# A graph kernel with attention: four attention tiles in one span of 68 nodes, softmax masks computed once

## The chip, the cores and the metric

The kernel runs on one core of a Trainium2 chip. The metric is the device time of one launch in microseconds (us), the median of several runs. The core has a matrix engine (PE; its weight loads are listed as PEld), VectorE (DVE), ScalarE (ACT), GpSimd (POOL) and SyncE (SP), each with its own instruction stream. SBUF is the working memory of 128 partitions, PSUM the memory that PE writes to.

## What is computed

A graph of 6250 nodes with 128 features and 100,000 edges, sorted by target, passes through a layer norm and two relational layers (RGCN), is added to the input, passes through a second layer norm and two attention layers (GAT) with batch norm and ELU, and is added again. The change concerns the attention layers:

```python
def _gat(x, src, dst, W, a_src, a_dst, b):        # H = 4 heads of FH = 32
    n = x.shape[0]
    xw = (x @ W).reshape(n, H, FH)
    al_s = jnp.einsum('nhf,hf->nh', xw, a_src)
    al_d = jnp.einsum('nhf,hf->nh', xw, a_dst)
    e = jax.nn.leaky_relu(al_s[src] + al_d[dst], NEG_SLOPE)
    m = jax.ops.segment_max(e, dst, num_segments=n)
    ee = jnp.exp(e - m[dst])
    den = jax.ops.segment_sum(ee, dst, num_segments=n)
    alpha = ee / den[dst]
    out = jax.ops.segment_sum(alpha[:, :, None] * xw[src], dst, num_segments=n)
    return out.reshape(n, H * FH) + b
...
loops = jnp.arange(n, dtype=edge_index.dtype)     # every node also has an edge to itself
src = jnp.concatenate([edge_index[0], loops])
dst = jnp.concatenate([edge_index[1], loops])
```

## The kernel before

**Tiles and chunks.** The 106,250 edges with self-loops, sorted by target, are cut into 832 tiles of 128 edges (`NT`), one edge a partition, and into 26 chunks of 32 tiles (`NCH`, `TC`). A table in device memory has a row for each node: 128 projected features and 2 x 4 attention terms (`DG` = 136 numbers). In `gat`, `gathers(k)` fetches the rows of a chunk's sources, one indirect DMA on POOL for each tile (L584), into two buffers of 16 tiles from the pool `grp` of seven.

**Sums.** `sums(k)` works through a chunk two tiles at a time, in 16 steps. `weight` (L917) multiplies the gathered rows of four tiles by their softmax weights `w`. `selections` (L601) makes for eight tiles a matrix of zeros and ones, 128 edges by a window of `W` = 24 nodes: `window == offset`, where `offset` is an edge's target less the first target of its tile. The matmul of rows and selection (L937) gives 128 features x 24 nodes in PSUM; `add` (L921) adds this to the running sum `self.sum` at a column that is known only at run time, so the first targets of the tiles (`base`, `start`) are read into VectorE's registers by `bases` (L589), 16 at a time. Before the first tile of a chunk the column of the node that is shared with the chunk before is corrected by the factor `shrink` (L930, L931). A tile that spans more than 24 nodes would need more passes of the loop in `layer`; their number (`passes_g`) is computed from the data.

**Softmax.** `softmax(k)` has a chunk as 128 partitions (4 heads x 32 tiles) by 128 edges. It copies the attention terms out of the gathered rows (ACT, L797), transposes them (L799), and finds each target's maximum and sum along the edges by scans in both directions. The masks for this are made anew in each chunk from `rows`, the targets as numbers: `cut` is 0 where neighbouring edges share the target and very negative else (L787 to L789), `same` is cut == 0 (L791), and `dr == dr[:, c]` finds the edges that share the target of the first or last edge of a tile (L823, L900). Targets that run over tile borders are joined by short scans over the 32 tiles on 4 partitions (L811 to L890), whose carries from chunk to chunk are copied into fresh tiles (`dl`, `ml`, `sc`). `own_tile` (L436, L437) picks for each partition the value of its own tile, by a product and a reduction.

**Order.** `in_order` fixes the traced order within DVE, ACT, PE and POOL. In the loop of `gat`, the gathers of chunk k+1 are issued ahead of the sums of chunk k, and the softmax of chunk k+1 is a generator whose steps are interleaved with the second half of the sums of chunk k: one step at step 3 (the masks) and one at each of the steps 7 to 15. So VectorE's queue has, behind the early half of the sums, the softmax of the next chunk, which waits for the last gather of that chunk.

**Lists.** `windows` and `chains` compute the graph's lists (`base`, `ahead`, the link masks) once. They run as steps between the halves of the first RGCN layer, as `early` in `run`. The RGCN layers have their own gathers (`htable`, 782 a layer, also L584), selections (L698, L703) and additions (L749).

Of the kernel before, what the change touches and what calls it, by code (L numbers as in the profile page):

```python
# [8 lines left out]
F32 = mybir.dt.float32  # L9
I32 = mybir.dt.int32  # L10
BF16 = mybir.dt.bfloat16
AF = mybir.ActivationFunctionType
# [32 lines left out]
NZ = -(-(N + 1) // W)  # L45
WG = 288
# [5 lines left out]
BIG = 1e30  # L52

# [14 lines left out]
class Gnn:  # L68
# [251 lines left out]
    order = staticmethod(lambda v: v.rearrange("o (c p) -> o p c", p=NP))  # L320
    by_tile = staticmethod(lambda v: v.rearrange("o (p c) -> o p c", c=SC))

    def windows(self, scratch):

        nc, const, dst = self.nc, self.const, self.dst
        order, by_tile = self.order, self.by_tile
        self.base = const.tile([1, NT], I32, name="base")
        nc.vector.tensor_copy(by_tile(self.base), order(dst[0:1, :]))  # L330
        self.ahead = const.tile([P, NT], F32, name="ahead")
        last, firsts, lasts = scratch[:, :NT], scratch[:, NT:2 * NT], scratch[:, 2 * NT:3 * NT + 1]
        flags = scratch[:, 4 * NT:6 * NT].rearrange("o (i t) -> o i t", i=2)
        for c in range(0, NT, NT // 2):
            w = slice(c, c + NT // 2)
            ps = self.ps()[:, :NT // 2]
            nc.tensor.matmul(ps, self.ones, dst[0:1, w], start=True, stop=True)
            nc.vector.scalar_tensor_tensor(self.ahead[:, w], ps, -1.0, dst[:, w], op0=ALU.mult, op1=ALU.add)
            ps = self.ps()[:, :NT // 2]
            nc.tensor.matmul(ps[:1, :], self.ident[:, P - 1:P], dst[:, w], start=True, stop=True)  # L340
            nc.vector.tensor_copy(last[:, w], ps[:1, :])
        yield
        nc.vector.tensor_copy(by_tile(firsts), order(dst[0:1, :]))
        nc.vector.memset(lasts[:, 0:1], -1.0)
        nc.vector.tensor_copy(by_tile(lasts[:, 1:]), order(last))
        nc.vector.tensor_tensor(flags[:, 0, :], firsts, lasts[:, :NT], ALU.is_equal)
        nc.vector.tensor_tensor(flags[:, 1, :], firsts, lasts[:, 1:], ALU.is_equal)

        nc.vector.tensor_sub(lasts[:, 1:], lasts[:, 1:], firsts)
        widest = scratch[:, 0:1]  # L350
        nc.vector.tensor_reduce(widest, lasts[:, 1:], AX.X, ALU.max)
        steps = self.small.tile([1, NZ], F32, name="steps", bufs=1)
        nc.vector.tensor_scalar(steps, self.steps, widest, None, op0=ALU.is_le)
        count = self.small.tile([1, 1], F32, name="count", bufs=1)
        nc.vector.tensor_reduce(count, steps, AX.X, ALU.add)
        passes = const.tile([1, 1], I32, name="passes")
        nc.vector.tensor_copy(passes, count)
        self.passes_g = passes
        yield

        self.both = const.tile([H, 2, NT], BF16, name="both")
        for i in range(2):
            for c in range(0, NT, NT // 2):
                w = slice(c, c + NT // 2)
                ps = self.ps()[:, :NT // 2]
                nc.tensor.matmul(ps[:H, :], self.ones[:, :H], flags[:, i, w], start=True, stop=True)
                nc.vector.tensor_copy(self.both[:, i, w], ps[:H, :])
        yield

    def chains(self, scratch):  # L370
# [3 lines left out]
        link, one = chunked(self.both[:, 0, :]), chunked(self.both[:, 1, :])  # L374
        self.link = link
        wide = [H, NCH, TC + 1]

        self.linkpen = const.tile(wide, BF16, name="linkpen")
        nc.vector.memset(self.linkpen, -BIG)
        lk = chunked(scratch[:H, NCH * P:NCH * P + NT])  # L380
        nc.vector.tensor_scalar(lk, link, 1.0, BIG, op0=ALU.subtract, op1=ALU.mult)
        nc.vector.tensor_copy(self.linkpen[:, :, :TC], lk)
# [3 lines left out]
        self.through = const.tile(wide, BF16, name="through")  # L386
        nc.vector.memset(self.through, 0.0)
        nc.vector.tensor_mul(self.through[:, :, 1:], link, one)
        self.throughpen = const.tile(wide, BF16, name="throughpen")
        nc.vector.tensor_scalar(self.throughpen, self.through, 1.0, BIG, op0=ALU.subtract, op1=ALU.mult)  # L390
        yield

        self.back = const.tile(wide, BF16, name="back")
        nc.vector.memset(self.back, 0.0)
        nc.vector.tensor_mul(self.back[:, :, :TC - 1], one[:, :, :TC - 1], link[:, :, 1:])
        self.apart = const.tile([H, NCH, TC], BF16, name="apart")
        nc.vector.tensor_scalar(self.apart, one, -1.0, 1.0, op0=ALU.mult, op1=ALU.add)
        self.backpen = const.tile(wide, BF16, name="backpen")
        nc.vector.memset(self.backpen, -BIG)
        nc.vector.tensor_scalar(self.backpen[:, :, :TC], one, 1.0, BIG, op0=ALU.subtract, op1=ALU.mult)  # L400
        nc.vector.tensor_add(self.backpen[:, :, :TC - 1], self.backpen[:, :, :TC - 1], self.linkpen[:, :, 1:TC])
        yield


        self.rows = const.tile([P, NCH, P], F32, name="rows")
        ri = scratch[:, :NCH * P].bitcast(I32).rearrange("p (k e) -> p k e", e=P)
        kv = self.keys[:NT * P].rearrange("(k t e) -> t k e", t=TC, e=P)
        for h in range(H):
            nc.sync.dma_start(ri[h * TC:(h + 1) * TC], kv)
        for k in range(0, NCH, 2):  # L410
            yield
            nc.vector.tensor_scalar(ri[:, k:k + 2], ri[:, k:k + 2], KDST, None, op0=ALU.logical_shift_right)
            nc.vector.tensor_scalar_mul(self.rows[:, k:k + 2], ri[:, k:k + 2], BIG)

# [805 lines left out]
```

## Time and profile before

| what | us |
|---|---|
| median of 3 runs (lowest, highest) | 4509.92 (4507.43, 4512.96) |
| the profiled execution: its time, its span | 4509.92, 4502.3 |
| gathers of RGCN layer one and two, first to last | 62.2 to 1050.0, 1086.4 to 2066.1 |
| gathers of attention layer one and two, first to last | 2165.5 to 3245.8, 3333.9 to 4415.5 |
| ACT, busy in all | 475.6 (11% of the span) |
| RECIPROCAL L895, one of 52 | 0.944 |
| DMA, mean share of 16 engines in 3334 to 3900 us | 0.23 |

The span is the time from the first to the last instruction of one profiled execution; the rest of its time lies around it. "Busy" adds up the time in which an engine executes. In the groups, a line of the program, an engine and an operation stand with their count, busy time and the mean of one, and behind the bar the engine's idle time just before them with what ended it. The granted clock of PE is 0.75 to 0.78 of full speed in the RGCN stretches and 0.50 in the attention.

### The profile page before, as it was taken

The numbers are of one execution on the slowest core, as the hardware profiler recorded it, in microseconds if no ns is written. First come the engines' busy times: TensorE is split into PE (matmuls) and PEld (weight loads), VectorE is DVE, ScalarE is ACT, GpSimd is POOL, SyncE is SP. The second block draws the span as 40 slices with busy tenths as digits, with TensorE's granted clock in tenths as the row PEclk, the third lists the DMA queues.
The fourth block names the chain that finished last, engine by engine and source line by source line (L and its number), as shares of the span: only waits on it lengthen the run. The fifth ranks groups of instructions, "written<-read, shape, count | busy, mean of one in ns | idle before, by whom it ended". The sixth has DMA issues, their size and how long they took to land. (4 is left out here: it accounts for less than half of the span.)

```text
span 4502.3 us, 41706 instructions
## 1 busy us (share of the span) xinstructions
PE 2645.9 (59%) x10042; PEld 2039.6 (45%) x10042; DVE 2567.8 (57%) x8572; ACT 475.6 (11%) x683; POOL 3153.1 (70%) x3242
## 2 busy tenths in 40 slices
PE   4888788887886888886244444444334344444434
PEld 3655555555555555554243333334323333333433
DVE  6556665554555555554365566556546556655656
ACT  3111110112110101102100000000030000000002
POOL 3777777775777777772577777777627777777771
PEclk8777787776777777777555555555555555555555
DMA  4221222222222222221222222222212222222221
GB/s 117 65 61 52 57 67 54 53 54 73 68 60 81 53 54 54 54 53 33 59 55 54 54 54 54 54 54 54 46 52 55 54 54 54 54 54 54 55 54 42
DMA packets 135172, 256.85 MB, mean 57 GB/s; under 512 B 56018, under 2 KB 76486, under 8 KB 134917
## 3 DMA queue, kind: packets, MB, share of 16 engines
q0 software_dynamic: 103296, 218.57, 19.9%
q1 hardware_dynamic: 31388, 34.67, 2.4%
q8 instruction: 88, 1.44, 0.1%
q14 instruction: 168, 1.37, 0.1%
q10 hardware_dynamic: 232, 0.80, 0.1%
HBM read 236.45 MB, written 17.37 MB: 56 GB/s over the span
## 5 line engine op out<-in xcount | busy, mean ns | idle before, releaser
L584 POOL DMA_INDIRECT v<-gtable,src_i x1664 | 1655.4, 995 | 694.0 <-issue 476.0
L584 POOL DMA_INDIRECT v<-htable,src_e x1564 | 1489.1, 952 | 567.7 <-issue 445.7
L740 PE MATMUL ps<-sw,v 128*128 128x192 f32 x3128 | 925.9, 423 | 293.2 <-DMA v<-htable,src_e 258.9
L740 PEld LDWEIGHTS ps<-sw,v 128*128 128x128 f32 x3128 | 587.6, 227 | 583.3 <-DMA v<-htable,src_e 303.8
L937 PE MATMUL ps<-sel,v 128*128 128x24 f32 x3328 | 772.1, 385 | 91.7 <-DVE v L917 65.4
L937 PEld LDWEIGHTS ps<-sel,v 128*128 128x128 f32 x3328 | 747.4, 330 | 139.5 <-DVE v L917 71.1
L749 DVE TENSOR_TENSOR part<-part,ps 128x192 f32 x1564 | 552.2, 353 | 272.2 <-PE ps L740 197.7
L711 PE MATMUL ps<-part,basis 128*128 128x288 f32 x1568 | 538.7, 511 | 2.3 <-DVE part L749 2.3
L799 PE MATMUL ps<-ident,sd 128*128 128x128 f32 x104 | 46.1, 475 | 768.4 <-ACT sd L797 768.4
L711 PEld LDWEIGHTS ps<-part,basis 128*128 128x128 f32 x1568 | 383.9, 252 | 122.8 <-issue 2.8
L804 DVE SCALAR_TENSOR_TENSOR own<-cut,ps 128x128 f32<-128x128 f32 x52 | 14.9, 287 | 657.5 <-PE ps L799 657.5
L706 ACT COPY part<-zero 128x2304 f32<-128x2304 f32 x100 | 210.9, 2111 | 1597.8 <-PE ps L711 1578.2
L799 PEld LDWEIGHTS ps<-ident,sd 128*128 128x128 f32 x104 | 19.0, 182 | 786.7 <-ACT sd L797 786.7
L921 DVE TENSOR_TENSOR acc<-acc,ps 128x24 f32 x1664 | 295.1, 177 | 101.4 <-PE ps L937 48.9
L703 DVE TENSOR_TENSOR sw<-sel,ps 128x1536 f32<-128x1536 f32 x196 | 343.7, 1754 | 13.0 <-DVE sel L698 0.2
L716 DVE TENSOR_TENSOR acc<-acc,ps 128x288 f32 x98 | 44.5, 454 | 458.3 <-PE ps L711 458.3
L917 DVE TENSOR_TENSOR v<-v,w 128x512 f32<-128x512 f32 x416 | 286.0, 687 | 5.0 <-ACT w L908 1.7
L797 ACT COPY sd<-v 128x64 f32<-128x64 f32 x208 | 53.0, 301 | 1162.6 <-DMA v<-gtable,src_i 1162.6
L430 PE MATMUL ps<-sel,head_of 128*4 128x32 f32 x208 | 44.6, 313 | 178.1 <-DVE sel L428 178.1
L892 PE MATMUL ps<-part,of_head 4*128 4x65 f32 x104 | 35.6, 443 | 171.1 <-DVE part L890 171.1
L691 PE MATMUL ps<-relT,of_tile 8*128 8x128 f32 x392 | 98.0, 331 | 51.7 <-DMA relT<-rels 51.7
L695 PEld LDWEIGHTS ps<-wc,hot 128*128 128x128 f32 x392 | 94.8, 260 | 40.0 <-DVE hot L692 39.7
(293 smaller groups left out, 2050.3 us busy)
## 6 DMA issues: line engine op xcount, KB each, us to landing
v<-gtable,src_i POOLq DMA_INDIRECT x1664, 2.6
v<-htable,src_e POOLq DMA_INDIRECT x1564, 2.5
gtable<-gtb SPq DMA_DIRECT2D x14, 476.0 KB
acc<-htable SPq DMA_DIRECT2D x24, 256.0 KB
htable<-x SPq DMA_DIRECT2D x7, 448.0 KB
relT<-rels SPq DMA_DIRECT2D x196, 4.0 KB
htable<-y SPq DMA_DIRECT2D x7, 448.0 KB
x<-in_x_dram SPq DMA_DIRECT2D x7, 441.0 KB
```

The source lines that it names most:

```text
L584: self.nc.gpsimd.indirect_dma_start(out=out, out_offset=None, in_=table, in_offset=bass.IndirectOffsetOnAxis(ap=idx, axis=0))
L691: nc.tensor.matmul(ps[:, :P], self.of_tile, rel.pop(h), start=True, stop=True)
L695: nc.tensor.matmul(coef[h][:, P:P + SC * NBASE], t, wc.rearrange("p g b -> p (g b)"), start=True, stop=True)
L703: nc.vector.tensor_tensor(x, s[:, :, None, :].to_broadcast(shape), c[:, :, :, None].to_broadcast(shape), ALU.mult)
L706: nc.scalar.copy(x, self.zero[:, :, None].to_broadcast([P, NBASE, WG]))
L711: nc.tensor.matmul(ps[:, :WG], bs[:, b, :], x[:, b, :], start=b == 0, stop=b == NBASE - 1)
L740: nc.tensor.matmul(ps[:, (j - i) * NBASE * W:(j - i + 1) * NBASE * W], v[:, i0 + j, :], sw[h][:, j].rearrange("p b w -> p (b w)"), start=T ...
L749: nc.vector.tensor_add(o, o, x.rearrange("p (b w) -> p b w", b=NBASE))
L799: nc.tensor.transpose(ps[:, i * P:(i + 1) * P], st.rearrange("p h t -> p (h t)"), self.ident)
L917: nc.vector.tensor_mul(x, x, wz[:, :, :, None].to_broadcast([P, Q, H, FH]))
L921: nc.vector.tensor_add(o, o, ps[:, j * W:(j + 1) * W])
L937: nc.tensor.matmul(ps[:, j * W:(j + 1) * W], v[i // G][:, i % G, :D], s[:, i % GD, :], start=True, stop=True)
```

## The change

1. A span of `WA` = 68 nodes takes the place of the 24-node window in the attention. Four tiles (`GQ`) share it: their offsets are counted from the first target of the four, their matmuls add up in one PSUM bank, and one addition of 128 x 68 follows them in place of four of 128 x 24. `weight` takes eight tiles at once instead of four; a selection is 8 x 68 wide. The registers are read once for a chunk, nine of them.
2. `cut`, `same`, `head` and `tail` are computed once for all chunks, in `chains`, as 16-bit floats and bytes, and kept; `softmax` reads them. `rows` and `rowlink` are no longer kept.
3. The chains over the tiles run on in one array (`ends`, 2 x 833 on 4 partitions): a chunk's scan starts from the element before it, with no copies of carries. The backward scans have two arrays in turn (`backs`). The two corrections at a tile's ends become one product.
4. `shrink` is copied by ACT. The softmax has nine steps instead of ten. The pool `grp` has six buffers instead of seven.

The diff, cut to its core:

```diff
+GQ = 4
+WA = 68
+NZA = -(-(N + 1) // WA)
...
     def windows(self, scratch):
...
+        for q in range(NQ):
+            first = dst[0:1, q * GQ * NP:(q * GQ + 1) * NP]
+            nc.vector.tensor_copy(self.base[:, :, q], first)
+            ps = self.ps()[:, :NP]
+            nc.tensor.matmul(ps, self.ones, first, start=True, stop=True)
...
+            nc.vector.tensor_sub(of_group(self.ahead[:, w]), of_group(dst[:, w]), ps[:, None, :].to_broadcast([P, GQ, NP]))
...
     def chains(self, scratch):
...
+        self.cut = tile("cut", P, P + 1)
+        self.same, self.head, self.tail = (tile(name, P, P, dtype=U8) for name in ("same", "head", "tail"))
...
         for k in range(0, NCH, 2):
+            z = slice(k, k + 2)
             yield
...
+            nc.vector.tensor_sub(self.cut[:, z, 1:P], rows[:, z, :P - 1], rows[:, z, 1:])
+            for mask, e in ((self.head, 0), (self.tail, P - 1)):
+                nc.vector.tensor_tensor(mask[:, z], rows[:, z], rows[:, z, e:e + 1].to_broadcast([P, 2, P]), ALU.is_equal)
...
+            nc.vector.tensor_scalar(self.same[:, z], self.cut[:, z, :P], 0.0, None, op0=ALU.is_equal)
...
+    def selections(self, g):
+
+        s = self.wide.tile([P, GD, WA], F32, name="selg")
         self.nc.vector.tensor_tensor(
-            s, self.window[:, None, :].to_broadcast([P, GD, W]),
-            self.offset[:, c:c + (GD - 1) * NP + 1:NP, None].to_broadcast([P, GD, W]), ALU.is_equal)
+            s, self.window[:, None, :].to_broadcast([P, GD, WA]),
+            self.offset[:, g:g + (GD - 1) * NP + 1:NP, None].to_broadcast([P, GD, WA]), ALU.is_equal)
...
     def softmax(self, k):
...
-        cut = self.soft.tile([P, P + 1], F32, name="cut")
-        nc.vector.tensor_copy(cut[:, 0:1], self.rowlink[:, k:k + 1])
-        nc.vector.memset(cut[:, P:], 0.0)
-        nc.vector.tensor_sub(cut[:, 1:P], dr[:, :P - 1], dr[:, 1:])
-        same = t("same")
-        nc.vector.tensor_scalar(same, cut[:, :P], 0.0, None, op0=ALU.is_equal)
-        yield
+        cut, same = self.cut[:, k, :], self.same[:, k, :]
...
-        nc.vector.tensor_copy(dl[:, 1:], cps[:H, :TC])
-        nc.vector.tensor_copy(dl[:, 0:1], carry[0])
...
+        nc.vector.tensor_tensor_scan(dc[:, past], ahead, cps[:H, :TC], dc[:, k * TC:k * TC + 1], op0=ALU.mult, op1=ALU.add)
...
-        nc.vector.tensor_scalar(e, dr, dr[:, 0:1], dcol, op0=ALU.is_equal, op1=ALU.mult)
-        nc.vector.tensor_add(e, e, d)
+        nc.vector.scalar_tensor_tensor(e, self.head[:, k, :], dcol, d, op0=ALU.mult, op1=ALU.add)
...
-        for i, c in enumerate((0, P - 1)):
-            self.own_tile(cols[:, i:i + 1], ps[:, i * TC:(i + 1) * TC])
-            nc.vector.tensor_scalar(inv, dr, dr[:, c:c + 1], cols[:, i:i + 1], op0=ALU.is_equal, op1=ALU.mult)
-            nc.vector.scalar_tensor_tensor(e, inv, 1.0, e, op0=ALU.add, op1=ALU.mult)
-        self.shrink = self.chain.tile([P, 1], F32, name="shrink")
-        nc.vector.tensor_copy(self.shrink, ps[:, 2 * TC:2 * TC + 1])
+        nc.scalar.copy(self.shrink, ps[:, 2 * TC:2 * TC + 1])
+        self.own_tile(cols, ps[:, :2 * TC].rearrange("p (i t) -> p i t", i=2))
+        nc.vector.tensor_scalar(inv, self.head[:, k, :], cols[:, 0:1], 1.0, op0=ALU.mult, op1=ALU.add)
+        nc.vector.scalar_tensor_tensor(inv, self.tail[:, k, :], cols[:, 1:2], inv, op0=ALU.mult, op1=ALU.add)
+        nc.vector.tensor_mul(e, e, inv)
...
     def sums(self, k, w, shrink):
...
+            x = v[t // G][:, t % G:t % G + GD, :D].rearrange("p t (h f) -> p t h f", h=H)
+            wz = w[:, :, t:t + GD].rearrange("p h t -> p t h")
+            nc.vector.tensor_mul(x, x, wz[:, :, :, None].to_broadcast([P, GD, H, FH]))
+        def add(i, ps):
+            o = self.sum[:, bass.ds(at[i], WA)]
+            nc.vector.tensor_add(o, o, ps[:, :WA])
         weight(0)
+        at = self.registers(self.start[0:1, k, :])
...
+            if t % GQ == 0:
+                ps = self.ps()
+            for i in range(t, t + 2):
+                nc.tensor.matmul(ps[:, :WA], v[i // G][:, i % G, :D], s[:, i % GD, :],
+                                 start=i % GQ == 0, stop=i % GQ == GQ - 1)
+            if t % GD == 0:
+                g = (k * TC + t) // GD + 1
+                if g < NT // GD:
+                    self.s = self.selections(g)
+                if t + GD < TC:
+                    weight(t + GD)
             if late:
                 add(*late)
-            late = (t, at, ps)
-            if t % G == G - 2:
+                late = None
+            if t % GQ == GQ - 2:
+                late = (t // GQ + 1, ps)
+            if t == TC - 2:
                 add(*late)
-                late = None
             yield
...
-                if step == 3 or step >= TC // 4 - 1:
+                if step >= TC // 4 - 1:
...
-        self.grp = self.pool("grp", 7)
+        self.grp = self.pool("grp", 6)
```

## The prediction

> **What bounds the kernel now.** I read the busy times first, then the costliest groups, the waits, the stretches of time, and last the timeline of one chunk.
>
> ```profile
> PE 2645.9 (59%) x10042; PEld 2039.6 (45%) x10042; DVE 2567.8 (57%) x8572; ACT 475.6 (11%) x683; POOL 3153.1 (70%) x3242
> ...
> L584 POOL DMA_INDIRECT v<-gtable,src_i x1664 | 1655.4, 995 | 694.0 <-issue 476.0 <-DVEq L589 187.5 <-ACT w L908 13.1
> ...
> L921 DVE TENSOR_TENSOR acc<-acc,ps 128x24 f32 x1664 | 295.1, 177 | 101.4 <-PE ps L937 48.9 <-DVE acc L921 2.4 <-issue 0.2
> L917 DVE TENSOR_TENSOR v<-v,w 128x512 f32<-128x512 f32 x416 | 286.0, 687 | 5.0 <-ACT w L908 1.7 <-DMA v<-gtable,src_i 0.7 <-issue 0.6
> ```
>
> The attention's gathers, 832 a layer, run on POOL at 0.94 us plus a 0.305 us issue gap, 1.249 us apart. They start at 2165.5 and end at 3245.8 us in layer one, 3333.9 to 4415.5 in layer two; inside these stretches POOL has no gap over 0.31 us. So it never waits for a buffer or another engine: POOL sets the pace, and the three engines that the change relieves wait for it.
>
> ```profile
> ACT sd L797 <- DMA v<-gtable,src_i: 1162.6, 103, 21.6
> POOL v L584 <- issue: 921.7, 3025, 0.3
> ```
> ```profile
> 2700.00:3246.00 546.00, 229.52 (x975) 205.83 (x975) 322.43 (x1404) 24.07 (x91) 418.09 (x420) 0.50 0.23 54
> 4415.00:4502.00 87.00, 36.87 (x156) 32.22 (x156) 56.95 (x183) 30.59 (x23) 0.54 (x1) 0.50 0.13 39
> ```
>
> The softmax waits 1162.6 us in all for the last landing of its chunk. In the middle of layer one DVE is busy 322 of 546 us, PE 230. Faster VectorE work is worth something only behind the last gather of a layer.
>
> Yet the gathers do hear VectorE: their mean is 995 ns, their floor 940. The timeline shows why.
>
> ```profile
> 2902.77 0.94 POOL L584 DMA_INDIRECT v<-gtable,src_i  x1 [0.30 <-issue]
> 2903.58 0.36 DVE L601 TENSOR_TENSOR sel<-window,offset 128x192 f32<-128x192 f32 x1 [1.03 <-issue]
> 2903.86 0.68 DVE L917 TENSOR_TENSOR v<-v,w 128x512 f32<-128x512 f32 x1
> 2904.01 1.34 POOL L584 DMA_INDIRECT v<-gtable,src_i  x1 [0.30 <-issue]
> ```
> ```profile
> 2936.76 0.94 POOL L584 DMA_INDIRECT v<-gtable,src_i  x1 [0.30 <-issue]
> 2936.87 0.34 DVE L601 TENSOR_TENSOR sel<-window,offset 128x192 f32<-128x192 f32 x1
> 2937.14 0.68 DVE L917 TENSOR_TENSOR v<-v,w 128x512 f32<-128x512 f32 x1
> 2938.01 0.94 POOL L584 DMA_INDIRECT v<-gtable,src_i  x1 [0.30 <-issue]
> 2938.12 0.69 DVE L917 TENSOR_TENSOR v<-v,w 128x512 f32<-128x512 f32 x1
> ```
>
> The gather of 2904.01 starts 0.15 us into a weighting and takes 0.40 us longer, its remaining 0.53 less 0.12; the gathers whose neighbours start after them stay at 0.94. I laid all 1664 gathers against VectorE's rows. A gather is held until 0.12 us before the end of the VectorE instruction running at its start, if that one began at least 0.045 us earlier and reads two SBUF tensors: L917 costs 66.5 us over both layers, L836 6.1, L601 4.9, L824 3.8, L896 3.7, in all 88. With an operand in PSUM nothing happens: 199 gathers started under L921 and 270 of the RGCN under the 1.754 us of L703, and lost under 1 us together. Behind a held L601 the gather slips in before L917.
>
> The Trainium skill, "SBUF — State Buffer", section "SBUF: two separate sides", has this as an exclusive lock on a port pair shared by VectorE and GpSimd: an operation with two SBUF inputs that starts first blocks the other for its whole length. It speaks against longer instructions, as the rows do. In its other direction (a gather would hold VectorE for 0.94 us) the rows differ: the L601 of 2936.87, inside a gather, takes its usual 0.34 us. By that half VectorE would lose time that it has to spare here, so the sum is the same.
>
> **The change, part by part.** 50 chunk periods count: 25 a layer have softmax and sums of one chunk under the gathers of the next.
>
> *Sums.* Adds: 1664 x 177 ns become 416 x about 0.225 (0.155 fixed + 68 x 1.04 ns, the slope from L703's 1536 elements in 1754 ns and L917's 512 in 687); they read PSUM and hold nobody. Matmuls: as many as before, L937 starts them 0.213 us apart, which is their weight load. 68 columns for 24 can cost nothing or, by the 136-column L958 (3.54 us for 14 at a clock near this one, 0.25 each), up to 0.03 x 64 = 2 us in each layer's tail; I take nothing. Weighting: half as many of 1024 elements, 0.687 + 512 x 1.04 ns = 1.22 us. Selections: as many, 544 elements, 0.361 + 352 x 1.04 ns = 0.725. Both read two SBUF tensors, so the gathers are held longer, by fewer instructions. What can hold a gather is the duration less 0.045 and 0.12: L917 0.52 us before, 1.05 after; selection 0.19 before, 0.56 after. At random phase one costs (window)²/(2 x 1.249): per chunk before 8 x 0.11 + 4 x 0.015 = 0.93 us, after 4 x 0.44 + 4 x 0.125 = 2.3. But the phase is not random: the last landing starts the chunk, and the gathers start 0.95 us (0.85 to 1.03) after its first operation L804, then every 1.249. A typical chunk's holds, in us after L804: 2.2 (0.38), 3.9 (0.09), 6.4 (0.15), 7.8 (0.48), 14.5 (0.08), 24.6 (0.39), 26.2 (0.24), in all 1.8, against 1.73 from the same grid laid over the rows' starts.
>
> So I lay the new order the same way, from L804. The softmax loses two copies (0.3), L823/L824 become one (0.4), a weighting and a selection become one selection (0.2), four small operations (0.3) and their adds (0.6) go, the two end corrections (2.1) become 1.4: the chunk's first weighting starts at 15.85 instead of 18.8. Then, with 0.6 us for 9 register loads (17 and 16 took 1.02 and 1.03), selection and weighting at 18.05/18.7, 20.0/20.6, 22.5/23.1. Holds: softmax 0.53 (with the selection at 7.06), first weighting 0.48, then 0.46, 0.57, 0.12: **2.16 us** a chunk. Against 1.73 that is +0.43 x 50 = **+22 us**. Moving the late part by 0.1 us moves this by 0.1, up to 2.65 at +0.5 us and down to 1.5 beyond it: that is the range, -11 to +46.
>
> *Softmax masks.* Removed with their writes from each chunk; head, tail and same read as bytes. No row reads bytes: between L791's 0.30 and L900's 0.52 us each; I take 0.30 to 0.35. All of it sits in VectorE's idle time (L804 alone waits 657.5 us for 52 starts, 12.6 a chunk). Without that cover it would be worth 2.9 us a chunk. The copy of the shrink factor on ACT, 0.15 to 0.31 us, lies beside the 0.94 us reciprocal L895.
>
> *Layer tails.* Behind the last gather of layer one, L804 starts at 3250.26, the first weighting at 3268.79, the last add ends at 3285.39. After: weighting at 15.85 for 18.53, but 0.53 longer, so the first matmul at 17.5; 64 matmuls at 0.22 (14.2 us of the 15.5 before, their stalls gone) and an add, 31.9 for 35.13: -3.3, twice **-6.6 us** (-2 to -10).
>
> *Building the masks*, in the RGCN's first layer: 39 new subtractions and comparisons of about 256 elements, 0.42 us and two SBUF inputs, hold (0.26)²/2.5 = 0.03 us each, 1 us; two conversions of 1664 elements 0 to 1.7 us each; the gathers there lose 13.1 us now, partly to steps that go. **+1 us** (-3 to +6). VectorE's own time there is hidden, POOL has no gap there either.
>
> *Six group buffers for seven.* Chunk k+2 needs those of k-1, whose sums end some 20 us into the gathers of k+1, half a chunk early: nothing. If that cover went, POOL would wait. In the batch norm the third exponential waits for the first block's matmuls, 3306.09 for 3306.07: 0.1 us, twice.
>
> *Span of 68.* The inputs are fixed by the seed: four tiles span at most 59 nodes, one tile at most 17, so one pass before and after.
>
> Sum: 4502.3 + 22 - 6.6 + 1 = 4519, and 7.6 us lie outside the span (4509.92 of this execution, also the median of the runs): **4527 us**.
>
> **Rivals.** (a) *The long weightings fall between the gathers.* If the first one starts over 0.5 us later than 15.85, the gather at 16.44 starts ahead of it and no other lies in it: 1.5 us a chunk, -11 - 6.6 + 1: 4493 us, faster. For it: a single 0.5 us in some twenty steps that I added up. Against: every earlier or equal start costs up to 2.65. (b) *Holds as before*, 1.65 to 1.9 a chunk: 4501 to 4512. For it: fewer instructions, same data. Against: the hold grows with the square of the length. (c) *Selection and weighting hold as one block* of 1.8 us, no gather slipping in: 1.1 us for each of three pairs in place of 0.4: +2 us a chunk over mine, 4600 to 4630. Against: it slips in before, in the 0.09 us between L601 and L917. (d) *VectorE's relief counts in full*, 2.9 us x 50: only if POOL weren't the bound; its gaps exclude it.
>
> **Numbers.** A measurement tells about 0.2%, 9 us, from no change. My case, with its own range of 4519 to 4565 (holds to 2.65 us, matmuls and masks at their upper ends): 0.49; (a) 0.26; (b) 0.14; (c) 0.11. So faster 0.26, same 0.14, slower 0.60. The range reaches past the middle of (a) and to the edge of (c): 4488 to 4590.
>
> **What would show it.** Right: mean gather of the table 1.003 to 1.02 us (995 now) with gaps of 0.305; stretched ones up to 2 us, under weightings of 1.22 and selections of 0.72; L804's wait longer; last landing to last add 3 us shorter. Wrong: a mean at or under 0.995, POOL gaps over 0.31 inside a layer (buffers), 1024 elements in much less than 1.2 us, or a hold under the adds.

## The result, and the profile after

| | before | after |
|---|---|---|
| median of the runs, us (lowest, highest) | 4510.41 (4507.24, 4515.56) | 4548.02 (4526.61, 4568.33) |
| runs | 15 | 12 |
| ratio, 95% interval | | 1.0081 (1.0062 to 1.0099) |
| the profiled execution: time, span, us | 4509.92, 4502.3 | 4561.75, 4560.0 |

The changed kernel is slower by 0.8%. Its twelve runs fall into two heaps of six, 4527 to 4540 and 4556 to 4568, and the median is the middle between them, a time that no run took; the lowest run is still 11 us above the highest of the kernel before. The profiled run is of the upper heap, so what the profile shows is some 14 us more than the median has. In the page's busy times and its costliest groups:

```profile
PE 2649.8 (58%) x9994; PEld 2030.5 (45%) x9994; DVE 2306.9 (51%) x6132; ACT 484.3 (11%) x735; POOL 3217.0 (71%) x3243
...
L596 POOL DMA_INDIRECT v<-gtable,src_i x1664 | 1717.0, 1032 | 691.7 <-issue 592.8
...
L909 DVE TENSOR_TENSOR v<-v,w 128x1024 f32<-128x1024 f32 x208 | 255.1, 1226 | 11.2 <-issue 8.2
...
L912 DVE TENSOR_TENSOR acc<-acc,ps 128x68 f32 x416 | 91.4, 220 | 131.2 <-PE ps L925 130.7
L608 DVE TENSOR_TENSOR selg<-window,offset 128x544 f32<-128x544 f32 x208 | 149.8, 720 | 0.1
```

VectorE has 2440 instructions and 261 us less to do, and the kernel is no faster for it: the 1664 gathers of the attention, still the pace, take 1032 ns each in place of 995. Their floor is 0.942 us; what a row of gathers has above 1664 x 0.942 = 1567.5 us is called *holds* below. That is 1655.4 - 1567.5 = 87.9 us before and 1717.0 - 1567.5 = 149.5 us after.

The stretches of time (columns as before: length, then busy time and count of PE, PEld, DVE, ACT, POOL, clock, DMA) show the tails behind the last gather of each layer and the middle of layer one:

```profile
3277.90:3362.40 84.50, 41.50 (x205) 37.64 (x205) 48.62 (x137) 37.71 (x32) 0.00 (x0) 0.62 0.11 42
4476.90:4560.00 83.10, 37.04 (x156) 32.05 (x156) 49.61 (x126) 30.85 (x24) 0.00 (x0) 0.50 0.13 41
2700.00:3246.00 546.00, 228.35 (x956) 200.43 (x956) 248.20 (x763) 25.50 (x101) 421.31 (x410) 0.50 0.23 53
```

The tails are shorter: 84.5 and 83.1 us, where there were 88.1 and 86.8. In the same 546 us of layer one, DVE's busy time falls from 322 to 248 us, and 410 gathers are made in place of 420. The books of the two profiled executions close: +61.6 holds - 7.3 tails + 3.1 (the first gather of the attention starts at 2168.6 us, not at 2165.5) - 5.8 (1.8 us outside the span in place of 7.6) = +51.6 us, of 4561.75 - 4509.92 = +51.8. POOL's gaps within the layers sum to 253.3 us in both kernels, none over 0.31 us.

Where the holds come from is seen in the timeline (start, duration, engine, line) at the start of one chunk's sums:

```profile
2997.80 1.23 DVE L909 TENSOR_TENSOR v<-v,w 128x1024 f32<-128x1024 f32 x1 [0.17 <-issue]
2998.12 1.72 POOL L596 DMA_INDIRECT v<-gtable,src_i  x1 [0.30 <-issue]
...
3000.09 0.16 DVE L916 TENSOR_TENSOR acc<-acc,snaps 128x1 f32 x1 [1.07 <-issue]
3000.15 0.95 POOL L596 DMA_INDIRECT v<-gtable,src_i  x1 [0.30 <-issue]
...
3000.42 0.72 DVE L608 TENSOR_TENSOR selg<-window,offset 128x544 f32<-128x544 f32 x1
3001.05 1.22 DVE L909 TENSOR_TENSOR v<-v,w 128x1024 f32<-128x1024 f32 x1
3001.40 1.69 POOL L596 DMA_INDIRECT v<-gtable,src_i  x1 [0.30 <-issue]
...
3002.96 1.22 DVE L909 TENSOR_TENSOR v<-v,w 128x1024 f32<-128x1024 f32 x1
3003.40 1.60 POOL L596 DMA_INDIRECT v<-gtable,src_i  x1 [0.30 <-issue]
```

Three weightings (L909) in a row have a gather beginning 0.32, 0.35 and 0.44 us into them, and each of these gathers takes 0.66 to 0.78 us too long: it ends 0.82 us after the weighting, that is its own 0.94 us after a point 0.12 us before the weighting's end. Over both layers, 120.6 of the 149.5 us of holds lie under L909. The gather of 3000.15 starts under the 0.16 us L916 and loses nothing.

### The profile page after: what moved, and what is told of

Its sections match the earlier page's. It is cut to its first block, busy times and chain, and to the rows that moved or that the text cites. A ratio compares the mean times of both kernels' runs of the same rounds, so it can differ in the third digit from the quotient of the medians.

```text
span 4560.0 us, 37619 instructions
## 1 busy us (share of the span) xinstructions
PE 2649.8 (58%) x9994; PEld 2030.5 (45%) x9994; DVE 2306.9 (51%) x6132; ACT 484.3 (11%) x735; POOL 3217.0 (71%) x3243
## 5 line engine op out<-in xcount | busy, mean ns | idle before, releaser
L596 POOL DMA_INDIRECT v<-gtable,src_i x1664 | 1717.0, 1032 | 691.7 <-issue 592.8
L748 PE MATMUL ps<-sw,v 128*128 128x192 f32 x3128 | 913.0, 420 | 298.1 <-DMA v<-htable,src_e 259.5
L925 PE MATMUL ps<-selg,v 128*128 128x68 f32 x3328 | 787.2, 422 | 92.2 <-issue 88.9
L925 PEld LDWEIGHTS ps<-selg,v 128*128 128x128 f32 x3328 | 743.1, 330 | 137.0 <-issue 120.5
L804 PE MATMUL ps<-ident,sd 128*128 128x128 f32 x104 | 46.1, 474 | 963.5 <-ACT sd L802 963.4
L809 DVE SCALAR_TENSOR_TENSOR own<-cut,ps 128x128 f32<-128x128 bf16 x52 | 14.9, 287 | 958.9 <-PE ps L804 958.9
L804 PEld LDWEIGHTS ps<-ident,sd 128*128 128x128 f32 x104 | 18.9, 181 | 985.6 <-ACT sd L802 985.6
L909 DVE TENSOR_TENSOR v<-v,w 128x1024 f32<-128x1024 f32 x208 | 255.1, 1226 | 11.2 <-issue 8.2
L912 DVE TENSOR_TENSOR acc<-acc,ps 128x68 f32 x416 | 91.4, 220 | 131.2 <-PE ps L925 130.7
L608 DVE TENSOR_TENSOR selg<-window,offset 128x544 f32<-128x544 f32 x208 | 149.8, 720 | 0.1
```

Of the source, the lines that this page charges most:

```text
L596: self.nc.gpsimd.indirect_dma_start(out=out, out_offset=None, in_=table, in_offset=bass.IndirectOffsetOnAxis(ap=idx, axis=0))
L608: self.nc.vector.tensor_tensor(s, self.window[:, None, :].to_broadcast([P, GD, WA]), self.offset[:, g:g + (GD - 1) * NP + 1:NP, None].to_b ...
L748: nc.tensor.matmul(ps[:, (j - i) * NBASE * W:(j - i + 1) * NBASE * W], v[:, i0 + j, :], sw[h][:, j].rearrange("p b w -> p (b w)"), start=T ...
L909: nc.vector.tensor_mul(x, x, wz[:, :, :, None].to_broadcast([P, GD, H, FH]))
L912: nc.vector.tensor_add(o, o, ps[:, :WA])
L925: nc.tensor.matmul(ps[:, :WA], v[i // G][:, i % G, :D], s[:, i % GD, :], start=i % GQ == 0, stop=i % GQ == GQ - 1)
```

## The experiments

The theory on trial: a VectorE instruction that reads two SBUF tensors holds a gather that starts while it runs, and how much that costs is decided by how long the instruction is and where it falls between the gathers. Rivals: the cost comes with VectorE's load as a whole, with the long weighting as such, or from other parts of the change (the span, the order of additions, the buffers).

### 1. One operand in PSUM

One bank of PSUM is kept aside (`kept`, the pool `psum` has seven for eight). In the first kernel the softmax weights are left there by the transposition, so that the weighting reads one tensor from SBUF and one from PSUM; their copy on ACT falls away. In the second the 68 numbers of `window` are copied there once, so that the selection reads only its offsets from SBUF. The third does both.

```diff
-        ps = self.ps()
-        nc.tensor.transpose(ps[:, :P], e, self.ident)
+        w = self.kept[:, :P].rearrange("p (h t) -> p h t", t=TC)
+        nc.tensor.transpose(self.kept[:, :P], e, self.ident)
...
-        w = self.soft.tile([P, H, TC], F32, name="w")
-        nc.scalar.copy(w.rearrange("p h t -> p (h t)"), ps[:, :P])
...
+        self.pwindow = self.kept[:, P:P + WA]
+        nc.vector.tensor_copy(self.pwindow, self.window)
...
-            s, self.window[:, None, :].to_broadcast([P, GD, WA]),
+            s, self.pwindow[:, None, :].to_broadcast([P, GD, WA]),
```

Weights in PSUM:

> The changed kernel, but the weighting reads the softmax weights from PSUM, where the transpose leaves them, and not from a copy in SBUF; same 1024 elements, same order. Theory (a gather is held by a VectorE operation with two SBUF tensors, for as long as it lasts): the 120.6 us that the profile of the changed kernel shows under the weightings go, the selections and the softmax keep some 20 to 60 us; mean gather of the attention table 0.96 to 0.98 us for 1.032; 4440 to 4480 us. Rival (what counts is a long VectorE operation on SBUF as such, or something else in the change, such as the wide span or the buffers): nothing changes, 4530 to 4570 us.

Window in PSUM:

> The changed kernel, but the 68-node window that the selections compare with lies in PSUM; the weightings are as they were. Theory: the selections, 0.72 us each, hold no gather any more (some 19 us of 149.6 in the profile), but a gather that they let pass can be caught by the weighting right behind: 4505 to 4570 us, with the holds under the weightings at 110 us or more. Rival (the holds go by an operation's length alone): the holds under the selections stay, 4530 to 4570 us.

Both:

> Both: weights and window in PSUM. Theory: only the softmax's own operations can hold a gather, some 0.3 us in each of 50 chunks, 10 to 30 us in all; mean gather 0.95 to 0.965 us; 4405 to 4445 us, faster than both kernels. Rival (length alone, or another part of the change): 4530 to 4570 us.

| | median, us (lowest, highest) | ratio to before, 95% | holds, us |
|---|---|---|---|
| weights in PSUM | 4445.73 (4440.15, 4449.18) | 0.9860 (0.9844 to 0.9877) | 39.0 |
| window in PSUM | 4516.46 (4512.95, 4525.06) | 1.0024 (1.0015 to 1.0034) | 105.3 |
| both | 4411.46 (4410.44, 4412.50) | 0.9788 (0.9771 to 0.9804) | 4.3 |

(The kernel before took 4506.16 us on that chip.) The groups of the kernel with both:

```profile
L597 POOL DMA_INDIRECT v<-gtable,src_i x1664 | 1571.8, 945 | 690.5 <-issue 602.6
...
L908 DVE TENSOR_TENSOR v<-v,kept 128x1024 f32<-128x1024 f32 x208 | 252.5, 1214 | 9.3 <-DMA v<-gtable,src_i 2.7
...
L609 DVE TENSOR_TENSOR selg<-kept,offset 128x544 f32<-128x544 f32 x208 | 149.4, 718 | 0.1
```

and its timeline at the start of a chunk's sums:

```profile
2983.44 1.22 DVE L908 TENSOR_TENSOR v<-v,kept 128x1024 f32<-128x1024 f32 x1
2984.47 0.94 POOL L597 DMA_INDIRECT v<-gtable,src_i  x1 [0.30 <-issue]
...
2986.72 1.21 DVE L908 TENSOR_TENSOR v<-v,kept 128x1024 f32<-128x1024 f32 x1
...
2986.97 0.94 POOL L597 DMA_INDIRECT v<-gtable,src_i  x1 [0.31 <-issue]
...
2988.21 0.94 POOL L597 DMA_INDIRECT v<-gtable,src_i  x1 [0.30 <-issue]
2988.61 1.22 DVE L908 TENSOR_TENSOR v<-v,kept 128x1024 f32<-128x1024 f32 x1
2989.46 0.94 POOL L597 DMA_INDIRECT v<-gtable,src_i  x1 [0.30 <-issue]
```

The weightings and selections are as long as before (1214 and 718 ns), the same engine does the same sums, and the gathers that start under them, at 2984.47 or 2986.97, take their 0.94 us. Of the gathers that start at least 45 ns into a weighting and 120 ns before its end, all 164 are held in the changed kernel, and none of 194 here. So neither the length of the instruction nor VectorE's load holds a gather; the second SBUF operand does. It is worth 136.6 us (4548.02 - 4411.46), close to the 145.2 us by which the holds fall in the profiles. Both parts are needed: with the window alone in PSUM the weightings still hold 101.1 us (110 or more were expected), and with the weights alone the selections hold 33.8.

The Trainium skill, "SBUF — State Buffer", section "SBUF: two separate sides", calls this an exclusive lock on a shared port pair: whichever of the two starts first, the VectorE operation with two SBUF inputs or a GpSimd operation that reads SBUF, keeps it for the whole instruction. The first half agrees with the 164 held gathers. The other half doesn't hold for the whole length of a gather: the L608 of 3000.42 in the changed kernel's timeline begins 0.27 us into the gather of 3000.15, which runs to 3001.10, and takes its usual 0.72 us. Only around a gather's start does VectorE lose anything. In the changed kernel 8 selections and 32 weightings begin between 0.006 us behind a gather's start and 0.031 us ahead of it; they hold no gather, and each takes 0.03 to 0.07 us longer than usual. With both operands in PSUM 38 selections begin in that place, and none takes over 0.002 us longer.

### 2. The weighting's width, in both kernels

In the changed kernel the weightings go back to four tiles each; in the kernel before they are widened to eight (`Q = 4` becomes `Q = 8`), with its 24-column window, its additions and its softmax as they were (the expectation calls the window 36 wide; it is 24).

```diff
-            x = v[t // G][:, t % G:t % G + GD, :D].rearrange("p t (h f) -> p t h f", h=H)
+            x = v[t // G][:, t % G:t % G + 4, :D].rearrange("p t (h f) -> p t h f", h=H)
...
-                if t + GD < TC:
-                    weight(t + GD)
+            if t % 4 == 0 and t + 4 < TC:
+                weight(t + 4)
```

The changed kernel with four:

> The changed kernel, but each weighting takes four tiles (512 elements, 0.69 us) as before the change, eight a chunk; span, selections, sums and masks as changed. Theory: what can hold a gather falls from 1.05 to 0.52 us for each, twice as many of them, and by the square rule to half in all: holds of 60 to 110 us for 149.6, 4475 to 4535 us. Rival (the wide selections, the accumulated sums or the six buffers cost the time): 4535 to 4565 us.

The kernel before with eight:

> The kernel before with its weightings made over eight tiles in place of four (1.22 us in place of 0.69 us, half as many), the span of 36, the additions and the selections as they were. Theory (what the change costs comes from weightings that are longer than the 0.945 us floor of a gather): the holds rise from 88 us by 15 to 60, less what falls away with half the weightings, so 4515 to 4570, about as much above before as the changed kernel. Rival (the coarse weighting is harmless by itself, and the span or the order of the additions is what costs): 4490 to 4512.

Measured: 4493.58 us (4490.98 to 4496.00), ratio 0.9970 (0.9959 to 0.9981), holds 80.4 us for the changed kernel with four; 4500.30 us (4498.22 to 4504.67), ratio 0.9987 (0.9978 to 0.9997), holds 83.9 us for the kernel before with eight. Undoing that one part makes the change a gain of 0.3%. But the same part in the kernel before costs nothing, against the expectation and inside its rival's range: wide weightings aren't dear by themselves. Its timeline shows why:

```profile
3015.84 1.22 DVE L917 TENSOR_TENSOR v<-v,w 128x1024 f32<-128x1024 f32 x1 [0.22 <-DMA v<-gtable,src_i]
3015.89 1.99 POOL L584 DMA_INDIRECT v<-gtable,src_i  x1 [0.30 <-issue]
...
3018.16 1.28 DVE L917 TENSOR_TENSOR v<-v,w 128x1024 f32<-128x1024 f32 x1
3018.18 0.94 POOL L584 DMA_INDIRECT v<-gtable,src_i  x1 [0.30 <-issue]
...
3021.46 1.22 DVE L917 TENSOR_TENSOR v<-v,w 128x1024 f32<-128x1024 f32 x1
3021.93 1.57 POOL L584 DMA_INDIRECT v<-gtable,src_i  x1 [0.30 <-issue]
```

The gather that starts 0.05 us into the first weighting loses 1.05 us. The second weighting begins 0.02 us ahead of its gather, too little to hold it. Over both layers the four weightings of a chunk hold 37.1, 4.6, 34.2 and 3.0 us: two of four fall clear. In the changed kernel the four hold 31.7, 38.4, 33.9 and 16.7. At random phase a weighting of 1.22 us would cost 1.055²/(2 x 1.249) = 0.45 us, and the 200 that have gathers beside them 89 us; the kernel before with eight has 79, the changed kernel 121.

### 3. Moving the weightings against the gathers

Reductions of 64 softmax weights, whose results aren't used, are put on VectorE ahead of a chunk's first weighting: two in the first kernel, six in the second. They read one SBUF tensor.

```diff
+        for i in range(6):
+            spare = self.chain.tile([P, 1], F32, name=f"spare{i}")
+            nc.vector.tensor_reduce(spare, w[:, 2 * (i % 2):2 * (i % 2) + 2, :].rearrange("p h t -> p (h t)"), AX.X, ALU.add)
         weight(0)
```

Two:

> The changed kernel with two 64-element reductions added on VectorE ahead of the first weighting of a chunk, which start the late half of the chunk 0.3 to 0.5 us later and compute nothing that is used. Theory (holds are a matter of where a weighting falls in the 1.249 us grid of the gathers): layout of the starts gives about 2.0 us of holds a chunk in place of 2.9, so the time falls by 20 to 45 us, to 4500 to 4530. Rival (more work on VectorE costs time, holds grow with it): 4545 to 4570 or above.

Six:

> The changed kernel with six 64-element reductions on VectorE between the last addition of a chunk and the first weighting of the next, whose results are not used. Two of them had left the first weighting where it was, 16.22 us into the chunk; six, 0.126 us apart, start it and all behind it 0.5 us later, at about 16.7 us. Theory (the holds are a matter of where the weightings fall between the gathers, which begin 0.92 us before that point): the gather that the first weighting holds for 0.67 to 0.77 us now begins ahead of it, and the layout of starts gives 2.1 us of holds a chunk in place of 2.9, so the holds in the profile fall from 150 us to 105 to 125 and the time to 4505 to 4530. Rival (holds grow with VectorE's work, wherever it falls): six more operations a chunk, 4548 to 4575.

With two the time is 4548.59 us (4541.10 to 4551.50), ratio 1.0084 (1.0067 to 1.0100), holds 136.8 us. This missed the theory's 4500 to 4530 and lies in the rival's range, but it decides nothing between them: the two run in the 0.17 us in which VectorE stands still ahead of the first weighting (the bracket of 2997.80 above), and the first weighting still starts 16.24 us after L809, the chunk's first operation, where it was 16.22. What the run does say is that 104 more VectorE instructions cost nothing that shows: 4548.59 against 4548.02 us.

With six the first weighting starts at 16.75 us, and the time is 4531.54 us (4529.70 to 4533.10), ratio 1.0056 (1.0039 to 1.0073), just above the 4505 to 4530 expected. The timeline of a chunk of the most frequent kind:

```profile
2987.90 1.21 DVE L909 TENSOR_TENSOR v<-v,w 128x1024 f32<-128x1024 f32 x1
2988.29 1.64 POOL L596 DMA_INDIRECT v<-gtable,src_i  x1 [0.30 <-issue]
...
2989.67 0.16 DVE L919 TENSOR_TENSOR acc<-acc,snaps 128x1 f32 x1 [0.56 <-DVE v L909]
...
2990.00 0.72 DVE L608 TENSOR_TENSOR selg<-window,offset 128x544 f32<-128x544 f32 x1
2990.23 1.31 POOL L596 DMA_INDIRECT v<-gtable,src_i  x1 [0.30 <-issue]
2990.64 1.22 DVE L909 TENSOR_TENSOR v<-v,w 128x1024 f32<-128x1024 f32 x1
...
2991.84 0.94 POOL L596 DMA_INDIRECT v<-gtable,src_i  x1 [0.30 <-issue]
```

The gather after the first hold now falls on the selection (0.23 us in, 0.37 lost), and the second weighting has none. The holds fall to 121.8 us, inside the 105 to 125 expected, and the profiled execution takes 4533.10 us: 27.7 us less holds, 28.65 us less time, for work that was added. In the medians the gain is 16.5 us, but the intervals of the two ratios overlap, and some runs of the changed kernel are as low, while its profiled run is of the upper heap. So it isn't shown that the six reductions make the kernel faster; what the two profiles show is that the time follows the holds.

The way there was not the one expected. The expectation had the first weighting rid of its gather, but it still holds one in 35 chunks, since the selection early in the chunk (after the softmax's first steps), which begins right at a gather's start, now holds nothing in most chunks, and that shifts all gathers behind it by 0.55 us. And the rest didn't move with the first weighting: the wait for the registers, ahead of L919, shrinks from 1.07 to 0.56 us, and the second and third weighting start at 19.48 and 21.38 us as before. Of the 50 chunks, 36 lose about 2 us and 14 about 3.2; the 14 are those in which the registers are read quickly (below, in the part on the size of the holds). In the changed kernel 33 lose 2.8 to 3.0 and 10 about 4.0. The 15 gathers that start under one of the reductions lose nothing.

### 4. The kernel before without its holds

The kernel before, with its weights and its 24-column window in PSUM (named 36 in the expectation):

> The kernel before with its softmax weights and its 36-node window read from PSUM, the sixteen-tile graph work otherwise untouched. Theory (the 88 us of holds in it come from the weightings and selections, which read two SBUF tensors): nearly all of them go, 4506 - 60 to 80 = 4425 to 4450, so that the change made on top of it (4411 with both in PSUM) is worth 15 to 40 us once the holds are gone. Rival (the holds follow VectorE's load, not its operands): 4490 to 4510.

Measured: 4426.84 us (4424.95 to 4428.96), ratio 0.9814 (0.9798 to 0.9830), holds 9.1 us:

```profile
L585 POOL DMA_INDIRECT v<-gtable,src_i x1664 | 1576.6, 947 | 697.4 <-issue 575.4
...
L916 DVE TENSOR_TENSOR v<-v,kept 128x512 f32<-128x512 f32 x416 | 283.6, 682 | 3.5 <-issue 1.2
```

The kernel before, too, lost 84 us (4510.95 on that chip - 4426.84) to its holds. With both kernels rid of them the change is a gain of 15.4 us by the medians, of two chips, or of 0.26% by the two ratios (0.9788 against 0.9814), 12 us.

### 5. Four runs on another chip

Four kernels ran on a chip where the kernel before itself took 5634.2 us (5556.2 to 5679.3) in the same rounds: the one with two reductions, the kernel before with its operands in PSUM and with eight-tile weightings, which were then run again elsewhere (2, 3 and 4 above), and the changed kernel with weightings of sixteen tiles.

> The changed kernel with two small VectorE reductions of 64 elements (one SBUF input, some 0.45 us together) put in front of each chunk's first weighting; nothing is left out. Theory with phases (the gathers keep their grid, a weighting that starts just behind a gather's start catches none): in the profile of the changed kernel the first weighting starts 16.3 us after the softmax's first operation and holds the gather of 16.55 for 0.77 us; 0.45 us later it starts behind that gather. Laid on the same grid, the chunk's holds fall from 2.9 to 2.0 us: 4500 to 4530 us, faster although work is added. Rival (holds are a share of VectorE's busy time, whatever the phase): 4545 to 4570 us.

> The kernel before with the softmax weights and the 24-node window in PSUM, nothing else. Theory: of the 88 us of holds, those under L917 and L601 go (71 us), some 10 to 25 us under the softmax stay: 4425 to 4450 us. Against the changed kernel with both in PSUM (4411 us) the rest is what the change is worth without its holds: 7 us of the two tails and the softmax's holds. Rival (the gain of the PSUM version needs the wide span and the precomputed masks): 4480 to 4510 us.

> The kernel before with one part of the change alone: weightings of eight tiles (1.22 us), four a chunk, in place of eight of 0.69 us. Theory: at random phase 4 x 0.445 + 0.3 is 2.1 us a chunk against 1.76 measured, by the phase 1.3 to 2.8: 4485 to 4560 us, with the holds under single weightings up to 1.05 us for 0.52. Rival (the longer weighting costs nothing, it was another part): 4500 to 4512 us with holds as before.

> The changed kernel with weightings of sixteen tiles (2048 elements, 2.29 us), two a chunk. Theory: what can hold is 2.12 us, more than the 1.249 us between two gathers, so each weighting holds one, for 0.9 to 2.1 us; 2 x 1.5 and 0.8 for the rest is 3.8 us a chunk, against 2.9: 4570 to 4615 us. Rival (the cost goes with the sum of the lengths, which falls from 4.9 to 4.6 us a chunk): 4535 to 4560 us.

They took 5234.31, 5901.69, 5516.26 and 5310.63 us, the kernel before with its operands in PSUM the longest, which elsewhere was among the shortest. In that kernel POOL waits 868.9 us in all for VectorE's additions, which it does in no profile from the other chips, and DVE's additions wait 955.4 us for something that the profile names only "remote". No verdict on the change is taken from these times. The holds can be read even so, as they follow from the gathers' own rows: 7.2 us for the kernel before with its operands in PSUM (9.1 on the other chip), 121.0 for two reductions (136.8), 98.8 for the kernel before with eight-tile weightings (83.9), and 191.5 us for sixteen-tile weightings, of which 177.9 under 96 weightings, up to 2.0 us each. What sixteen tiles do to the time of an undisturbed run stays untried.

### One sum for all

If the holds are all that tells these kernels apart, the profiled execution's time less its holds must be the same for every kernel of a family:

| kernel | time, us | holds, us | rest, us |
|---|---|---|---|
| changed | 4561.75 | 149.5 | 4412.2 |
| two reductions | 4546.32 | 136.8 | 4409.5 |
| six reductions | 4533.10 | 121.8 | 4411.3 |
| window in PSUM | 4512.95 | 105.3 | 4407.7 |
| weightings of four | 4493.44 | 80.4 | 4413.0 |
| weights in PSUM | 4449.18 | 39.0 | 4410.2 |
| both in PSUM | 4412.50 | 4.3 | 4408.2 |
| before | 4509.92 | 87.9 | 4422.0 |
| before, weightings of eight | 4500.31 | 83.9 | 4416.4 |
| before, both in PSUM | 4428.96 | 9.1 | 4419.9 |

While the times of the changed kernel's family differ by 149 us, the rest stays within 5.3 us of one another, at 4410 on the mean; that of the kernel before is 6 to 12 us higher, some of it time outside the span (last section). That is the change: a gain of some 10 us, and a loss of what the gathers are held longer.

## Why the prediction was right, and by how much it was off

**The bound** was right. POOL's gaps sum to 253.3 us before and after, and 261 us less VectorE work bought nothing under the gathers. The rival in which the relief counts in full is excluded by that. The wait of the softmax's first operation grew as foreseen, from 657.5 us (L804) to 958.9 (L809).

**The mechanism** was right: the gathers are slowed by VectorE instructions with two SBUF tensors, and not by those with an operand in PSUM (experiment 1). The durations too: 1.22, 0.725 and 0.225 us were foreseen for weighting, selection and addition, and 1.226, 0.720 and 0.220 measured.

**The size of the holds** was the term that was off: +22 us foreseen, +61.6 in the profiled execution, and about +48 in the median run (4548.0 - 4509.9, with the 7.3 of the tails and the 5.8 outside the span added and the 3.1 ahead of the attention taken off). By its parts, in us a chunk, measured over 50 chunks:

| | foreseen | profiled |
|---|---|---|
| softmax and its selection (and all others) | 0.53 | 0.58 |
| first weighting | 0.48 | 0.63 |
| second | 0.46 | 0.77 |
| third | 0.57 | 0.68 |
| fourth | 0.12 | 0.33 |
| sum | 2.16 | 2.99 |

The mean gather, 1.032 us in the profile, is accordingly above the 1.003 to 1.02 given as a sign of being right.

Two steps of the layout did it. The first weighting was put at 15.85 us after the chunk's first operation and starts at 16.22: taking steps out of the softmax brought 2.6 us where 2.95 were summed up. By the prediction's own slope of 0.1 us for each 0.1 us, 0.37 us makes +18, and 4527 + 18 = 4545; that this is nearly the median proves little, as the second step comes on top and no run lies between 4540 and 4556.

The second step is the register read, put at 0.6 us because there are nine values in place of 16. The read itself stands in the trace (DVEq is VectorE's sequencer; shortest, median and longest in ns), first for the kernel before, then for the changed one:

```profile
L589 DVEq TENSOR_LOAD <-start x104: 1095/1099/1117, 2225.3 to 4447.1; - x104
```
```profile
L601 DVEq TENSOR_LOAD <-start x56: 843/2064/3418, 2166.1 to 4497.3; - x56
```

(Four of the 56, of 2.9 us and more, read 13 values ahead of a layer's first chunk.) So nine values take longer than 16 did: 2.06 us in 38 of the 52 chunks, and 0.85 in the other 14, which are each fourth chunk of a layer, from its first on. (Nine values of 4 bytes are 36 bytes a chunk, so that each fourth chunk's lie a multiple of 16 bytes behind the first; that this is the cause is a guess, which no run tests.) The read runs beside the first weighting. Behind that, VectorE stands still for 1.07 us in the 38 chunks and not at all in the 14, and neither is the 0.6 laid out.

This sets the later weightings. After a hold, the gathers start again 0.12 us before the weighting's end and then every 1.249 us, so 1.13 and 2.38 us after it. In the timeline above, one of the 38, the second weighting starts 2.02 us after the first one's end (3001.05 against 2999.03), so the gather is 0.35 us into it; at 1.63 us, as laid out, it would have been 0.75 us in. In the 14 it starts 0.88 us after it, with the gather 0.25 us in. The fourth begins 2.20 us after the third's end in the 14 and holds a gather in each of them, for 0.9 us; in the others it begins 1.12 us after it, right at a gather's start, and holds one in four chunks of 36.

Where a start falls right beside a gather's, a very small shift decides. In the changed kernel's profile a gather that starts 0.018 to 0.031 us into the selection early in the chunk isn't held; one that starts 0.035 to 0.061 us into it (the prediction had 0.045 as the least) is, for about 0.55 us, in 29 of the 50 chunks. These lose 3.0 us in all with the long register read and 4.0 with the short one, the others 2.5 and 2.9. It fits that the runs vary by 42 us where those of the kernel with both operands in PSUM vary by 2; but no run of the lower heap was profiled, so this cause of the two heaps is argued, not shown.

**Tails, masks, buffers, span.** -6.6 us foreseen for the tails, -7.3 measured. Ahead of the attention +1 foreseen, +3.1 measured, within the -3 to +6 given. Six buffers: no gap on POOL, as foreseen. The part outside the span was taken as 7.6 us, and is 1.8.

**The rivals.** That the long weightings fall between the gathers was given 0.26 if the first started over 0.5 us later than 15.85: the kernel with six reductions starts it 0.9 us later, and has 2.4 us a chunk in place of 1.5, since the gathers' grid and the later weightings moved otherwise; 4531.5 us, not 4493. That the holds stay as before is excluded for the changed kernel (149.5 against 87.9), but it is what the width of the weightings alone did in the kernel before (83.9), though the hold "grows with the square of the length", which at random phase would have made it 8 x (0.44/2 - 0.11) x 50 = 44 us dearer. One block of selection and weighting would have shown holds of up to 1.8 us; the longest were 1.0. That the change came out slower, and not even, owes something to chance: the same widening cost nothing at the phase of the kernel before, and the layout that was to fix the phase put the first weighting 0.4 us and the next two 0.8 us too early.

## What to carry to other kernels

Where indirect gathers on POOL set the pace, look at which VectorE instructions read two SBUF tensors, and leave one of the operands in PSUM, best one that PE makes anyway: here this is worth 1.9% to the kernel before and 3.0% to the changed one, whose 4411.46 us beats both, while the rest of the change was worth some 10 us. An instruction may not be priced by its length alone beside a periodic engine, but by where it starts within the period, and that start must be followed through the waits in front of it (here a register read) to within a tenth of a us. Time less holds, computed for every variant, tells in one column whether a mechanism explains all.

## What the runs showed of the hardware that was not expected

- Reading nine values into VectorE's registers took 2.06 us in 38 chunks and 0.85 us in 14, where 16 took 1.10. What makes the difference wasn't tried.
- A VectorE instruction with two SBUF operands that begins right at a gather's start takes 0.03 to 0.07 us longer (40 in the changed kernel); one that begins later in the gather loses nothing.
- The time of an execution outside its span is 7.5 to 8.6 us for the kernel before, 1.7 to 1.9 us for the changed kernel and its variants save that with sixteen-tile weightings (4.5 to 5.7), 1.8 to 1.9 us for the kernel before with its operands in PSUM, and 4.6 to 6.9 us for it with eight-tile weightings. What makes this difference wasn't found.
- On one chip the same kernel took 5634 us in place of 4510, at nearly the same granted clock (0.61 to 0.62 against 0.63), and the order of the variants was turned round.
